# One adaLN-plus-cross-attention block: cross-attention values computed beside their own sequence, a new stage end, maxima spread by transposing a repeated column

## The chip, the cores and the metric

The kernel runs on one core of a Trainium2 chip. The metric is device time in microseconds, the median over several executions. TensorE does the matmuls and transposes, VectorE (DVE), ScalarE (ACT) and GpSimd (POOL) the elementwise work, SyncE (SP) issues most of the DMAs.

## The reference, cut to what matters

All arithmetic is float32. x has 16 sequences of 224 tokens, width 512; the context has 750 rows for each sequence; there are 16 heads of 32.

```
c_proj = silu(c) @ W_mod + b_mod                     # six rows of 512 for each sequence
shift_a, scale_a, gate_a, shift_m, scale_m, gate_m = split(c_proj, 6)
x_norm = _ln(x) * (1 + scale_a) + shift_a
q, k, v = split(x_norm @ W_qkv + b_qkv, 3)
x = x + gate_a * (softmax(q k^T * scale) v @ W_proj + b_proj)        # self-attention
q_c = _ln(x) @ W_qc + b_qc
k_c, v_c = split(_ln(context) @ W_kvc + b_kvc, 2)
x = x + (softmax(q_c k_c^T * scale) v_c @ W_cproj + b_cproj)         # cross-attention
h = gelu((_ln(x) * (1 + scale_m) + shift_m) @ W_mlp1 + b_mlp1)
x = x + gate_m * (h @ W_mlp2 + b_mlp2)
```

## The kernel before

Every engine executes its instructions in the order in which the program writes them (class Ordered), so the order of the source is the order of each queue. Tile waits for what an instruction reads or overwrites.

The program has three stages one after the other.

1. **Self-attention**, by pairs of sequences. Before it, the six conditioning parts are made from W_mod by `make_part` (line 279). Parts 0 and 1 are made before the first pair; parts 2 to 5 from slots of the plan of the first pair. For the shifts and scales it computes columns directly: for each of four output chunks and four input chunks a matmul with 128 weight columns and 16 moving columns (the profile shows two instructions for each f32 matmul). For the gates it uses c_t as weights, 16 columns, and moves 512 columns of W_mod. Parts 0 and 1 lie between c_act (the Silu of the conditioning) and the first transposes of x.

2. **Cross-attention**, by units (b, g): sequence b, group g of four heads. A unit computes scores of its six context chunks (125 rows each) in three steps; a step fills the four PSUM banks of `ps_s`, DVE keeps a running maximum in `top` and ACT copies the scores to `pt` (`keep`, line 991), which frees the banks. At the end of the unit `maxima` (line 1004) transposes `top` and reduces it to negated maxima m. One unit later the maxima are spread over the rows and added to `pt` (`subtract`, line 1031), ACT takes the exponential and POOL adds up the sums `acc` (`weights`, line 1043). Two units later the values are multiplied (`values`, line 1058) and normalized (`finish`). The spread is done so: POOL splits m into three bf16 pieces in `nmc` (`split_max`, line 122), TensorE transposes them to rows (`max_row`, line 1022), ACT copies the rows to `mrow`, and a bf16 matmul with ones puts them on all 125 partitions.

Between these steps TensorE does the other work of the stage from a plan. `at_slot(b, g, slot, f)` (line 907) puts a piece of work into one of six slots of a unit: slots 0 and 1 follow the first scores (the spread of the first half lies between them), slots 2 and 3 the second scores (the spread of the second half lies between them), slots 4 and 5 the third scores; then come the maxima of this unit, and at the start of the next unit the values of the unit before the last. The pieces are: `project_k` for the next group (slots 0 and 1), `project_q` (slot 5, in group 1 slot 3), `project_v` (values of one context chunk; chunks 0 to 3 one sequence ahead, 4 and 5 in the sequence itself), `turn_ctx` (transposes of the next sequence's context), `turn_x`, and `project` (the output projection of the sequence before, in slot 4 of groups 1 and 3). The last sequence also loads, normalizes and transposes the first rows for the MLP (`mlp_load`, `mlp_norm`, `mlp_turn`) and loads its first weights (`mlp_begin`).

After the last unit a hand-written end (lines 1106 to 1128) runs the last values, four plain MLP products, the last spread and exponentials, and the last projection.

3. **MLP**, in blocks of 512 rows, with sums of weight quarters (`mlp_sums`, line 691, and `sums_2`, line 1144) made once, while the first block runs; `First` (line 747) and `second` do the two products.

Three PSUM banks (`ps_mm`) serve all the pieces in turn, one (`ps_o`) serves the spread and the values.

Of the kernel before, what the change touches and what calls it, by code (L numbers as in the profile page):

```python
# [37 lines left out]
def kernel(  # L38
# [73 lines left out]

# [6 lines left out]
    nmc = const.tile([TP, HG, TC, P], BF16, name="nmc")  # L119
    nc.gpsimd.memset(nmc, 0.0)  # L120

    def split_max(engine, nm, m):

        r = small.tile(list(m.shape), F32, name="rest")
        engine.tensor_copy(nm[:, :, :, 0], m)
        engine.tensor_tensor(r, m, nm[:, :, :, 0], ALU.subtract)
        engine.tensor_copy(nm[:, :, :, 1], r)
        engine.tensor_tensor(nm[:, :, :, 2], r, nm[:, :, :, 1], ALU.subtract)
# [9 lines left out]
    for off, vec in ((o_mod, b_mod), (o_qkv, b_qkv), (o_qc, b_qc), (o_kvc, b_kvc), (o_mlp, b_mlp1)):  # L138
        rows = vec.shape[0] // P
        nc.scalar.dma_start(out=brow[off : off + rows, :], in_=vec.rearrange("(r p) -> r p", p=P))  # L140
# [113 lines left out]
    wq, wk, wv = (load_w(ws, w_qkv[:, i * H : (i + 1) * H], f"wqkv{i}") for i in range(3))  # L254
    bg = mp.tile([B, 2, H], F32, name="bg", bufs=1)
# [4 lines left out]
    c_act = mp.tile([B, H], F32, name="c_act", bufs=1)  # L260
    nc.scalar.activation(c_act, c_in, AF.Silu)
# [7 lines left out]
    ps = ps_mm.tile([P, 512], F32, name="mm")  # L269
    turn(ps[:, :nbias], brow, ident[:nbias, :nbias])  # L270
    nc.vector.tensor_copy(bcol, ps[:, :nbias])
    for i in (1, 4):
        sl = bcol[:, o_mod + i * KC : o_mod + (i + 1) * KC]
        nc.vector.tensor_scalar(sl, sl, 1.0, None, ALU.add)

    bqc = const.tile([P, KC], F32, name="bqc")
    nc.vector.tensor_scalar(bqc, bcol[:, o_qc : o_qc + KC], SCALE, None, ALU.mult)

    def make_part(i):
        w = w_part[i]  # L280
        ps = ps_mm.tile([P, 512], F32, name="mm")
        if i % 3 == 2:
            for k in range(KC):
                mm(ps[:B, :H], c_t[:, k, :], w[:, k, :], start=(k == 0), stop=(k == KC - 1))
            g = mp.tile([B, H], F32, name="gates", bufs=1)
            nc.vector.tensor_tensor(g, ps[:B, :H], bg[:, i // 3, :], ALU.add)
            nc.sync.dma_start(out=gate_d[i // 3], in_=g)
        else:
            slot = (i // 3) * 2 + i % 3
            for m in range(KC):  # L290
                for k in range(KC):
                    mm(
                        ps[:, m * B : (m + 1) * B], w[:, k, m * P : (m + 1) * P], c_t[:, k, :],
                        start=(k == 0), stop=(k == KC - 1),
                    )
            for m in range(KC):
                nc.vector.tensor_scalar(
                    mod_t[:, slot * KC + m, :], ps[:, m * B : (m + 1) * B],
                    bcol[:, o_mod + i * KC + m : o_mod + i * KC + m + 1], None, ALU.add,
                )  # L300
# [133 lines left out]
    if True:  # L434
# [70 lines left out]
        for p in range(NP):  # L505
            if p < NP - 1:
                for g in range(1, KC):
                    at_slot(p, 2 * g - 2, 0, lambda p=p, g=g: whole(project_qk(p, g)))
                    at_slot(p, 2 * g - 2, 1, lambda p=p, g=g: whole(project_qk(p, KC + g)))
                for t in range(PT if p else 0):  # L510
                    at_slot(p, 1 + t // 2 * 2, t % 2, lambda p=p, t=t: whole(project(p - 1, t)))
            else:

                left = [(project_qk, p, m) for m in (1, KC + 1, 2, KC + 2)]
                left += [(project, p - 1, t) for t in range(2)]
                left += [(project_qk, p, m) for m in (3, KC + 3)]
                left += [(project, p - 1, t) for t in range(2, PT)]
                parts = [h for f, *args in left for h in halves(lambda f=f, args=args: f(*args))]
                for i, h in enumerate(parts):
                    at_slot(p, i // 3, i % 3 // 2, h)  # L520
            if p == 0:
                at_slot(p, 1, 0, lambda: make_part(2))
                at_slot(p, 1, 1, lambda: make_part(3))
                at_slot(p, 1, 1, lambda: load_part(4))
                at_slot(p, 1, 1, lambda: load_part(5))
                at_slot(p, 3, 0, lambda: make_part(4))
                at_slot(p, 3, 1, lambda: make_part(5))
                at_slot(p, 3, 1, load_cross)
            n = p + 1
            if n < NP:  # L530
                if n > 1:
                    at_slot(p, 0, 0, lambda n=n: fetch(n))
                at_slot(p, 1, 0, lambda n=n: norm_begin(n))
                for t in range(PT):
                    at_slot(
                        p, 1 + t // 2, t % 2, lambda n=n, t=t: norms[PB * n + t // TC].stats(t % TC)
                    )
                for j in range(PB):
                    at_slot(p, 1 + j, 1, lambda n=n, j=j: norms[PB * n + j].apply())
                for k in range(KC):  # L540
                    at_slot(p, 4, k // 2, lambda n=n, k=k: turn_x(n, k))
                for t in range(PT):
                    at_slot(p, 5 + t // 2, t % 2, lambda n=n, t=t: project_v(n, t))
                at_slot(p, 7, 0, lambda n=n: whole(project_qk(n, 0)))
                at_slot(p, 7, 1, lambda n=n: whole(project_qk(n, KC)))

        def self_scores(p, g, j, nm):
# [15 lines left out]
            split_max(nc.vector, nm, m)  # L563
# [33 lines left out]
        make_part(0)  # L597
        make_part(1)
# [212 lines left out]
    with tc.tile_pool(name="ca", bufs=2, reuse_waits="tile") as ca:  # L811
# [98 lines left out]
        for b in range(B):  # L910
            n = b + 1
            for g in range(KC):
                f, m = (b, g + 1) if g < KC - 1 else (n, 0)
                if f < B:
                    for hf in range(2):
                        at_slot(b, g, hf, lambda f=f, m=m, hf=hf: project_k(f, m, hf))
                    at_slot(b, g, (5, 3, 5, 5)[g], lambda f=f, m=m: project_q(f, m))
            if b:
                at_slot(b, 1, 4, lambda b=b: project(b - 1, 0))
                at_slot(b, 3, 4, lambda b=b: project(b - 1, 1))  # L920
            else:
                for c in range(4):
                    at_slot(0, c // 2, 3 + c % 2, lambda c=c: project_v(0, c))
                at_slot(0, 2, 0, make_bcproj)
            at_slot(b, 0, 2, lambda b=b: project_v(b, 4))
            at_slot(b, 0, 4, lambda b=b: project_v(b, 5))
            if n < B:

                for c in range(CH):
                    at_slot(b, 0, 3 if b else 5, lambda n=n, c=c: turn_ctx(n, c))  # L930
                    at_slot(b, 2, 3, lambda n=n, c=c: turn_ctx(n, CH + c))
                for c, (u, slot) in enumerate(((1, 2), (2, 2), (2, 4), (3, 3))):
                    at_slot(b, u, slot, lambda n=n, c=c: project_v(n, c))
                for k in range(0, KC, 2):
                    at_slot(b, 3, 2, lambda n=n, k=k: turn_x(n, k))
# [5 lines left out]
            if n == B:  # L941
# [7 lines left out]
                for c, (u, slot) in enumerate(((2, 4), (2, 5), (3, 1), (3, 2))):  # L949
                    at_slot(b, u, slot, lambda c=c: mlp_turn(ps_mm, c))  # L950
            if b + 2 < B:
                for hf in range(2):
                    at_slot(b, 2 * hf, 3 if b or hf else 5, lambda b=b, hf=hf: load_ctx(b + 2, hf))
                    for c in range(CH):
                        at_slot(
                            b, 1 + 2 * hf, (4, 5, 5)[c] - hf, lambda b=b, hf=hf, c=c: cnorms[b + 2, hf].stats(c)
# [7 lines left out]
        class Unit:  # L964
# [39 lines left out]
            def maxima(self):  # L1004
                m = small.tile([TP, HG, TC], F32, name="mc")
# [14 lines left out]
                split_max(nc.gpsimd, nmc, m)  # L1020

            def max_row(self):
                ps = ps_mm.tile([P, 1024], BF16, name="mm")
                for s in range(HG):
                    for c in range(TC):
                        lo = s * N + c * TP
                        turn(ps[:, lo : lo + TP], nmc[:, s, c, :], ident16[:TP, :TP])
                self.row = ca.tile([P, HG * N], BF16, name="mrow", bufs=1)
                nc.scalar.copy(self.row, ps[:, : HG * N])

            def subtract(self, h):

                bc = ps_o.tile([P, 512], F32, name="o")
                mm(
                    bc[:CP, : 2 * N], ones16[:, :CP], self.row[:, 2 * h * N : 2 * (h + 1) * N],
                    start=True, stop=True,
                )
# [5 lines left out]
            def weights(self, h):  # L1043

                if h == 0:
# [12 lines left out]
            def values(self):  # L1058
# [7 lines left out]
                sums(self.o, [self.acc], CP)  # L1066
# [18 lines left out]
        for b, g in units:  # L1085
# [3 lines left out]
            for n in range(CH):  # L1089
                st = cur.scores(n)  # L1090
                if n == 0 and prev:
                    prev.max_row()
# [16 lines left out]
        cur.max_row()  # L1109
# [3 lines left out]
        cur.weights(0)  # L1113
        mlp_plain(sc[:, 2], 2)
        cur.subtract(1)
        cur.weights(1)
        mlp_plain(sc[:, 3], 3)
        mlp_turned(nc.vector)
        mlp_sums(nc.vector, mlp["in"], 1)
# [3 lines left out]
        cur.finish()  # L1123
        ahead = First(1)
# [7 lines left out]
    with tc.tile_pool(name="ml", bufs=3, reuse_waits="tile") as ml:  # L1132
# [32 lines left out]
        with (  # L1165
# [82 lines left out]
            for q in range(NG):  # L1248
# [64 lines left out]
```

## Time and profile before

| | |
|---|---|
| Runs before | 2943.93, 2943.95, 2952.13 us; median 2943.95 us |
| Profiled execution | 2940.97 us; span 2939.2 us; mean granted TensorE clock 0.991 |
| PE busy | 2850.1 us, 97% of the span |
| DVE, ACT, POOL busy | 65%, 40%, 44% |
| Cross-attention of sequences 1 to 14 | 854 to 2122 us of the span |
| Last sequence, stage end, first MLP block | 2122 to 2294 us |

Nearly every instruction is recorded under line 28, that of a helper, so groups are told apart by the names of their tiles: `mm<-ident,nmc` is a transpose of nmc into an mm bank. TensorE rows show the weights' partitions and columns (128*125), then the moving operand. In a timeline the columns are start, length from the first start to the last end, engine, operation, tiles, shapes, count, and in brackets the idle time before it and who ended it. Matmuls overlap, so the price of a group is the distance to the start of the next one, not its length.

### The profile page before, as it was taken

To read this page: it belongs to the slowest core of one execution; us is meant where nothing else is said; L and a number is where in the kernel's file an instruction comes from. 1 tells how busy PE (TensorE), PEld (TensorE's weight loads), DVE (VectorE), ACT (ScalarE), POOL (GpSimd) and SP (SyncE) were. 2 spreads that over 40 slices of the span, in tenths; PEclk is the share of its full clock that TensorE was granted. 3 is DMA by queue.
4 is the path that set the end of the run, shared out by engine and by line. 5 is a ranking of instruction groups with operands and counts; after the bars stand their busy time and mean duration, and the time that the engine had idled before them with its cause. 6 is when DMAs were issued, how large, how long until landed. Compare 5 with 4: busy or idle time off the path is not lost.

```text
span 2939.2 us, 46558 instructions
## 1 busy us (share of the span) xinstructions
PE 2850.1 (97%) x19389; PEld 1829.9 (62%) x19389; DVE 1913.6 (65%) x2688; ACT 1175.4 (40%) x1462; POOL 1296.2 (44%) x1636
## 2 busy tenths in 40 slices
PE   8999999998999999999999999999978999999999
PEld 5544444444555565555656555555545888888888
DVE  3677766676478778777787777777775643443343
ACT  1222222221466665666566656665653022112211
POOL 1022222122367666676666766666564510221021
PEclk9999999999999999999999999999989999999999
DMA  5111110100100010100101100000012101111110
GB/s 189 59 32 32 32 32 11 59 11 26 54 32 24 22 35 24 34 28 19 34 24 34 35 18 28 26 33 24 22 44 99 55 30 49 43 47 30 54 44 29
DMA packets 55383, 114.40 MB, mean 39 GB/s; under 512 B 4308, under 2 KB 4372, under 8 KB 55172
## 3 DMA queue, kind: packets, MB, share of 16 engines
q1 hardware_dynamic: 54560, 110.58, 11.7%
q8 instruction: 152, 2.49, 0.4%
q10 hardware_dynamic: 612, 0.85, 0.1%
q14 instruction: 59, 0.48, 0.1%
HBM read 89.33 MB, written 22.09 MB: 38 GB/s over the span
## 4 chain that ended last, share of the span: by engine, by line
PE 80%; DVE 8%; issue 4%; ACT 4%; POOL 3%; DMA 1%; SPq 0%; ACTq 0%; POOLq 0%; DVEq 0%
PE mm L28 46%; PE a L28 10%; PE sc L28 9%; PE o L28 8%; PE b L28 5%; ACT pt L28 3%; PE c L28 3%; DVE at L28 2%; DVE top L28 2%; POOL acc L28 1%; DVE stats L28 1%; DVE m L28 1%; DVE mc L28 1%; ACT kt L28 1%; DMA gate<-gate_d 1%
## 5 line engine op out<-in xcount | busy, mean ns | idle before, releaser
L28 POOL TENSOR_TENSOR acc<-acc,pt 125x448 f32<-125x448 f32 x512 | 584.3, 1141 | 40.2
L28 DVE TENSOR_TENSOR pt<-pt,o 125x896 f32<-125x896 f32 x384 | 394.4, 1082 | 92.0 <-PE o L28 87.0
L28 ACT COPY pt<-sc 125x1792 f32<-125x1792 f32 x192 | 317.4, 1653 | 223.3 <-DVE top L28 199.0
L28 DVE TENSOR_TENSOR top<-top,sc 125x896 f32<-125x896 f32 x320 | 346.7, 1084 | 40.6 <-PE sc L28 34.0
L28 PE MATMUL mm<-wkvc,cxt 128*125 128x512 f32 x768 | 354.4, 604 | 8.6 <-ACT kt L28 8.6
L28 POOL TENSOR_TENSOR upd<-upd,gate 112x512 f32<-112x512 f32 (+1 forms) x60 | 78.9, 1315 | 632.5 <-DVE upd L28 627.8
L28 PE MATMUL mm<-cxt,wkvc 128*128 128x375 f32 x1024 | 350.5, 484 | 2.4 <-ACT cxt L28 2.4
L28 ACT ACTIVATE pt<-pt 125x896 f32<-125x896 f32 x384 | 339.1, 955 | 12.9 <-DVE pt L28 12.2
L28 POOL TENSOR_TENSOR acc<-pt 125x448 f32<-125x448 f32 x128 | 146.5, 1144 | 382.6 <-ACT pt L28 382.6
L28 DVE RECIPROCAL at<-o 128x224 f32<-128x224 f32 x128 | 198.8, 1553 | 102.1 <-PE o L28 102.1
L28 PEld LDWEIGHTS mm<-cxt,wkvc 128*128 128x128 f32 x1024 | 190.4, 191 | 112.7 <-issue 13.3
L28 PEld LDWEIGHTS mm<-wkvc,cxt 128*125 128x125 f32 x768 | 136.5, 187 | 175.2 <-issue 153.5
L28 ACT ACTIVATE pt<-sc 112x1792 f32<-112x1792 f32 x64 | 106.6, 1665 | 343.4 <-PE sc L28 338.8
L28 POOL TENSOR_TENSOR rstd<-mv,eps 112x2 f32<-112x2 f32 (+3 forms) x93 | 17.8, 192 | 475.5 <-DVE mv L28 475.5
L28 PE MATMUL sc<-qt,kt 32*125 32x224 f32 x3072 | 201.6, 377 | 12.9 <-ACT pt L28 12.3
L28 PE MATMUL mm<-xt,wqkv 128*128 128x448 f32 x512 | 209.0, 551 | 4.7 <-DVE xt L28 4.7
L28 DVE TENSOR_REDUCE m<-sc 112x8 f32<-112x1792 f32 x64 | 129.6, 2026 | 120.3 <-PE sc L28 120.3
L28 PEld LDWEIGHTS sc<-qt,kt 32*125 32x125 f32 x3072 | 132.9, 183 | 92.6 <-issue 41.0
L28 ACT COPY mrow<-mm 128x896 bf16<-128x896 bf16 x64 | 58.0, 906 | 309.2 <-PE mm L28 309.2
L28 PE MATMUL o<-pt,vt 125*32 125x224 f32 x3072 | 158.6, 355 | 0.0
L28 PEld LDWEIGHTS mm<-xt,wqkv 128*128 128x128 f32 x512 | 92.3, 190 | 86.7 <-issue 80.9
L28 ACT COPY mx<-a 128x512 f32<-128x512 f32 x26 | 15.3, 587 | 325.0 <-POOL upd L28 306.3
(192 smaller groups left out, 4846.7 us busy)
## 6 DMA issues: line engine op xcount, KB each, us to landing
cx<-in_ctx_dram SPq DMA_DIRECT2D x96, 250.0 KB
x<-in_x_dram SPq DMA_DIRECT2D x16, 448.0 KB
x_self<-x SPq DMA_DIRECT2D x16, 448.0 KB
x<-x_self SPq DMA_DIRECT2D x16, 448.0 KB
x_cross<-x SPq DMA_DIRECT2D x16, 448.0 KB
mx<-x_cross SPq DMA_DIRECT2D x28, 256.0 KB
w<-in_L_xcond_W_mlp_dram SPq DMA_DIRECT2D x7, 1024.0 KB
xr<-x_cross SPq DMA_DIRECT2D x28, 256.0 KB
```

What stands on the lines that cost most here:

```text
L28: return lambda *args, **kw: self.tc.keep_in_program_order(f(*args, **kw))
```

## The change

- **Spread of the maxima.** `nmc`, the split on POOL and `max_row` go. `subtract` transposes, for each head and token chunk, the f32 column of m repeated 125 times straight into the `ps_o` bank: four transposes for each half.
- **Plan of cross-attention.** project_v of chunks 1 to 5 is done in its own sequence: group 0 slots 2, 3, 4 and group 1 slots 2, 4; only chunk 0 stays one sequence ahead (group 3 slot 4). The context is turned in group 1 slot 3 and group 2 slot 3 (before: group 0 slot 3 and group 2 slot 3), and its loads and statistics move with it. The output projection of the sequence before is in slot 2 of groups 2 and 3. project_q is in slot 5 of every group. turn_x goes to slot 3. The last sequence has its own places for the projection (group 3 slots 0 and 2) and for the MLP's transposes.
- **Stage end.** The last unit doesn't sum on POOL: TensorE sums all six pieces of pt with ones. The MLP's `mlp_turned` and `mlp_sums` on DVE come after the last unit's values and normalization, and no longer before.
- **MLP start.** `mlp_sums` of quarter 3 goes to POOL; that of quarter 0 goes from POOL to DVE, into the second product of the first block.
- **Conditioning.** The shifts and scales are computed as rows (c_t as weights, 512 columns of W_mod moved), copied by ACT and transposed in four small transposes. c_in is the first DMA on ACT's queue; the bias rows are loaded after the Silu.

The diff, cut to its core:

```diff
-    def make_part(i):
-        w = w_part[i]
+    def part_rows(i):
+
         ps = ps_mm.tile([P, 512], F32, name="mm")
+        for k in range(KC):
+            mm(ps[:B, :H], c_t[:, k, :], w_part[i][:, k, :], start=(k == 0), stop=(k == KC - 1))
+        if i % 3 < 2:
+            r = mp.tile([B, H], F32, name="part", bufs=2)
+            nc.scalar.copy(r, ps[:B, :H])
+            return r
+        return ps
+
+    def finish_part(i, ps):
...
             slot = (i // 3) * 2 + i % 3
+            rows, ps = ps, ps_mm.tile([P, 512], F32, name="mm")
             for m in range(KC):
-                for k in range(KC):
-                    mm(
-                        ps[:, m * B : (m + 1) * B], w[:, k, m * P : (m + 1) * P], c_t[:, k, :],
-                        start=(k == 0), stop=(k == KC - 1),
-                    )
+                turn(ps[:, m * B : (m + 1) * B], rows[:, m * P : (m + 1) * P], ident[:B, :B])
...
-        make_part(0)
-        make_part(1)
+        rows = [part_rows(i) for i in range(2)]
+        make_columns()
+        for i in range(2):
+            finish_part(i, rows[i])
...
-                    at_slot(b, g, (5, 3, 5, 5)[g], lambda f=f, m=m: project_q(f, m))
+                    at_slot(b, g, 5, lambda f=f, m=m: project_q(f, m))
             if b:
-                at_slot(b, 1, 4, lambda b=b: project(b - 1, 0))
-                at_slot(b, 3, 4, lambda b=b: project(b - 1, 1))
+                for c, (u, slot) in enumerate(((2, 2), (3, 2)) if n < B else ((3, 0), (3, 2))):
+                    at_slot(b, u, slot, lambda b=b, c=c: project(b - 1, c))
             else:
-                for c in range(4):
-                    at_slot(0, c // 2, 3 + c % 2, lambda c=c: project_v(0, c))
-                at_slot(0, 2, 0, make_bcproj)
-            at_slot(b, 0, 2, lambda b=b: project_v(b, 4))
-            at_slot(b, 0, 4, lambda b=b: project_v(b, 5))
+                at_slot(0, 0, 2, lambda: project_v(0, 0))
+                at_slot(0, 2, 2, make_bcproj)
+            for c, (u, slot) in enumerate(((0, 2), (0, 3), (0, 4), (1, 2), (1, 4))):
+                at_slot(b, u, slot, lambda b=b, c=c + 1: project_v(b, c))
             if n < B:
                 for c in range(CH):
-                    at_slot(b, 0, 3 if b else 5, lambda n=n, c=c: turn_ctx(n, c))
+                    at_slot(b, 1, 3, lambda n=n, c=c: turn_ctx(n, c))
                     at_slot(b, 2, 3, lambda n=n, c=c: turn_ctx(n, CH + c))
-                for c, (u, slot) in enumerate(((1, 2), (2, 2), (2, 4), (3, 3))):
-                    at_slot(b, u, slot, lambda n=n, c=c: project_v(n, c))
+                at_slot(b, 3, 4, lambda n=n: project_v(n, 0))
                 for k in range(0, KC, 2):
-                    at_slot(b, 3, 2, lambda n=n, k=k: turn_x(n, k))
+                    at_slot(b, 3, 3, lambda n=n, k=k: turn_x(n, k))
...
-                for c, (u, slot) in enumerate(((2, 4), (2, 5), (3, 1), (3, 2))):
+                for c, (u, slot) in enumerate(((2, 2), (2, 3), (2, 4), (3, 4))):
                     at_slot(b, u, slot, lambda c=c: mlp_turn(ps_mm, c))
             if b + 2 < B:
                 for hf in range(2):
-                    at_slot(b, 2 * hf, 3 if b or hf else 5, lambda b=b, hf=hf: load_ctx(b + 2, hf))
+                    at_slot(b, 1 + hf, 3, lambda b=b, hf=hf: load_ctx(b + 2, hf))
                     for c in range(CH):
                         at_slot(
-                            b, 1 + 2 * hf, (4, 5, 5)[c] - hf, lambda b=b, hf=hf, c=c: cnorms[b + 2, hf].stats(c)
+                            b, 2 + hf, (4, 5, 5)[c] - hf, lambda b=b, hf=hf, c=c: cnorms[b + 2, hf].stats(c)
                         )
...
             def subtract(self, h):
                 bc = ps_o.tile([P, 512], F32, name="o")
-                mm(
-                    bc[:CP, : 2 * N], ones16[:, :CP], self.row[:, 2 * h * N : 2 * (h + 1) * N],
-                    start=True, stop=True,
-                )
+                for s in range(2):
+                    for c in range(TC):
+                        lo = s * N + c * TP
+                        col = self.m[:, 2 * h + s, c : c + 1].to_broadcast([TP, CP])
+                        turn(bc[:CP, lo : lo + TP], col, ident[:TP, :TP])
...
-                sums(self.o, [self.acc], CP)
+                if self.acc is None:
+                    sums(self.o, [pt[:, :, j * N : (j + 1) * N] for pt in self.pts for j in range(2)], CP)
+                else:
+                    sums(self.o, [self.acc], CP)
...
         mlp_plain(sc[:, 0], 0)
-        cur.max_row()
         prev.finish()
         mlp_plain(sc[:, 1], 1)
         cur.subtract(0)
-        cur.weights(0)
+        cur.weights(0, False)
         mlp_plain(sc[:, 2], 2)
         cur.subtract(1)
-        cur.weights(1)
+        cur.weights(1, False)
         mlp_plain(sc[:, 3], 3)
-        mlp_turned(nc.vector)
-        mlp_sums(nc.vector, mlp["in"], 1)
         for m in range(KC):
             gelu(sc[:, m], mlp["h"][0][:, m], m)
         cur.values()
         cur.finish()
+        mlp_turned(nc.vector)
+        mlp_sums(nc.vector, mlp["in"], 1)
...
-                    mlp_sums(nc.vector, ml, 3)
+                    mlp_sums(nc.gpsimd, ml, 3)
                     sums_2()
                     first(3)
-                    mlp_sums(nc.gpsimd, ml, 0)
...
+                    if (i, half, p) == (GC, 0, 3):
+                        mlp_sums(nc.vector, ml, 0)
```

More of the change, by code (lines that the diff above doesn't have):

```diff
@@ L117, with split_max @@
         nms.append(t)
-    nmc = const.tile([TP, HG, TC, P], BF16, name="nmc")
-    nc.gpsimd.memset(nmc, 0.0)
-    def split_max(engine, nm, m):
+    def split_max(nm, m):
         r = small.tile(list(m.shape), F32, name="rest")
[L125 to L128, printed above, removed]
+        nc.vector.tensor_copy(nm[:, :, :, 0], m)
+        nc.vector.tensor_tensor(r, m, nm[:, :, :, 0], ALU.subtract)
+        nc.vector.tensor_copy(nm[:, :, :, 1], r)
+        nc.vector.tensor_tensor(nm[:, :, :, 2], r, nm[:, :, :, 1], ALU.subtract)
     o_mod, o_qkv = 0, 6 * KC
@@ L137 @@
     brow = const.tile([nbias, P], F32, name="brow")
-    for off, vec in ((o_mod, b_mod), (o_qkv, b_qkv), (o_qc, b_qc), (o_kvc, b_kvc), (o_mlp, b_mlp1)):
-        rows = vec.shape[0] // P
-        nc.scalar.dma_start(out=brow[off : off + rows, :], in_=vec.rearrange("(r p) -> r p", p=P))
     bcol = const.tile([P, nbias], F32, name="bcol")
@@ L254 @@
     wq, wk, wv = (load_w(ws, w_qkv[:, i * H : (i + 1) * H], f"wqkv{i}") for i in range(3))
+    c_act = mp.tile([B, H], F32, name="c_act", bufs=1)
+    nc.scalar.activation(c_act, c_in, AF.Silu)
+    for off, vec in ((o_mod, b_mod), (o_qkv, b_qkv), (o_qc, b_qc), (o_kvc, b_kvc), (o_mlp, b_mlp1)):
+        rows = vec.shape[0] // P
+        nc.scalar.dma_start(out=brow[off : off + rows, :], in_=vec.rearrange("(r p) -> r p", p=P))
     bg = mp.tile([B, 2, H], F32, name="bg", bufs=1)
@@ L258 @@
         nc.scalar.dma_start(out=bg[:, i, :], in_=b_mod[lo : lo + H].partition_broadcast(B))
-    c_act = mp.tile([B, H], F32, name="c_act", bufs=1)
-    nc.scalar.activation(c_act, c_in, AF.Silu)
     c_t = mp.tile([P, KC, B], F32, name="c_t", bufs=1)
@@ L267, with make_columns @@
     nc.vector.tensor_copy(c_t.rearrange("p k b -> p (k b)"), ps[:, : KC * B])
[L269 to L274, printed above, removed]
     bqc = const.tile([P, KC], F32, name="bqc")
-    nc.vector.tensor_scalar(bqc, bcol[:, o_qc : o_qc + KC], SCALE, None, ALU.mult)
-    def make_part(i):
-        w = w_part[i]
+    def make_columns():
         ps = ps_mm.tile([P, 512], F32, name="mm")
+        turn(ps[:, :nbias], brow, ident[:nbias, :nbias])
+        nc.vector.tensor_copy(bcol, ps[:, :nbias])
+        for i in (1, 4):
+            sl = bcol[:, o_mod + i * KC : o_mod + (i + 1) * KC]
+            nc.vector.tensor_scalar(sl, sl, 1.0, None, ALU.add)
+        nc.vector.tensor_scalar(bqc, bcol[:, o_qc : o_qc + KC], SCALE, None, ALU.mult)
+    def part_rows(i):
+        ps = ps_mm.tile([P, 512], F32, name="mm")
+        for k in range(KC):
[6 more added lines that the diff above has]
+    def finish_part(i, ps):
         if i % 3 == 2:
-            for k in range(KC):
-                mm(ps[:B, :H], c_t[:, k, :], w[:, k, :], start=(k == 0), stop=(k == KC - 1))
             g = mp.tile([B, H], F32, name="gates", bufs=1)
@@ L289, in make_part @@
             slot = (i // 3) * 2 + i % 3
+            rows, ps = ps, ps_mm.tile([P, 512], F32, name="mm")
             for m in range(KC):
-                for k in range(KC):
-                    mm(
-                        ps[:, m * B : (m + 1) * B], w[:, k, m * P : (m + 1) * P], c_t[:, k, :],
-                        start=(k == 0), stop=(k == KC - 1),
-                    )
+                turn(ps[:, m * B : (m + 1) * B], rows[:, m * P : (m + 1) * P], ident[:B, :B])
             for m in range(KC):
@@ L521, with part @@
             if p == 0:
-                at_slot(p, 1, 0, lambda: make_part(2))
-                at_slot(p, 1, 1, lambda: make_part(3))
+                made = {}
+                def part(i):
+                    made[i] = part_rows(i)
+                    if i % 3 == 2:
+                        finish_part(i, made[i])
+                at_slot(p, 1, 0, lambda: part(2))
+                at_slot(p, 1, 1, lambda: part(3))
                 at_slot(p, 1, 1, lambda: load_part(4))
                 at_slot(p, 1, 1, lambda: load_part(5))
-                at_slot(p, 3, 0, lambda: make_part(4))
-                at_slot(p, 3, 1, lambda: make_part(5))
+                at_slot(p, 2, 0, lambda: finish_part(3, made[3]))
+                at_slot(p, 3, 0, lambda: part(4))
+                at_slot(p, 3, 1, lambda: part(5))
+                at_slot(p, 3, 1, lambda: finish_part(4, made[4]))
                 at_slot(p, 3, 1, load_cross)
@@ L562, in self_scores @@
             )
-            split_max(nc.vector, nm, m)
+            split_max(nm, m)
         def self_weights(p, g, j, row):
@@ L1004, in maxima @@
             def maxima(self):
-                m = small.tile([TP, HG, TC], F32, name="mc")
+                self.m = m = small.tile([TP, HG, TC], F32, name="mc")
                 for h in range(2):
@@ L1019, in maxima, with subtract @@
                     )
[L1020 to L1024, printed above, removed]
+            def subtract(self, h):
+                bc = ps_o.tile([P, 512], F32, name="o")
+                for s in range(2):
                     for c in range(TC):
                         lo = s * N + c * TP
[L1027 to L1033, printed above, removed]
-                mm(
-                    bc[:CP, : 2 * N], ones16[:, :CP], self.row[:, 2 * h * N : 2 * (h + 1) * N],
-                    start=True, stop=True,
-                )
+                        col = self.m[:, 2 * h + s, c : c + 1].to_broadcast([TP, CP])
+                        turn(bc[:CP, lo : lo + TP], col, ident[:TP, :TP])
                 less = bc[:CP, : 2 * N].rearrange("p (s t) -> p s t", s=2).unsqueeze(2)
@@ L1041, in subtract, with weights @@
                     nc.vector.tensor_tensor(w4, w4, less.to_broadcast([CP, 2, 2, N]), ALU.add)
-            def weights(self, h):
+            def weights(self, h, add=True):
+                if not add:
+                    for pt in self.pts:
+                        w = pt[:, 2 * h : 2 * h + 2, :]
+                        nc.scalar.activation(w, w, AF.Exp)
+                    self.acc = None
+                    return
                 if h == 0:
@@ L1090 @@
                 st = cur.scores(n)
-                if n == 0 and prev:
-                    prev.max_row()
                 if n == 0 and last:
```

## The prediction

> **What bounds the kernel now.** The page first: is one engine the bound over the whole span?
>
> ```profile
> PE 2850.1 (97%) x19389; PEld 1829.9 (62%) x19389; DVE 1913.6 (65%) x2688; ACT 1175.4 (40%) x1462; POOL 1296.2 (44%) x1636
> ```
>
> TensorE is. So a change pays only where it takes work from TensorE, ends one of its waits, or keeps its clock up. Where its idle time lies is in the table by stretches (columns: stretch, its length, busy us of PE, PEld, DVE, ACT, POOL, granted clock, DMA share, GB/s):
>
> ```profile
> 750.00:854.00 104.00, 98.76 (x642) 57.04 (x642) 64.88 (x87) 53.00 (x63) 52.21 (x75) 0.98 0.12 38
> 854.00:2122.00 1268.00, 1250.10 (x9530) 751.55 (x9532) 976.27 (x1137) 783.09 (x924) 869.71 (x1114) 1.00 0.08 26
> 2122.00:2217.60 95.60, 75.85 (x608) 46.12 (x600) 72.99 (x98) 49.57 (x51) 57.66 (x72) 0.89 0.15 49
> 2217.60:2255.50 37.90, 30.65 (x134) 15.46 (x131) 21.92 (x20) 10.90 (x13) 15.24 (x14) 0.91 0.04 13
> 2255.50:2294.00 38.50, 34.66 (x154) 29.99 (x153) 22.57 (x22) 12.46 (x27) 22.34 (x10) 0.96 0.60 200
> ```
>
> These are cross-attention of sequence 0, of 1 to 14, of 15, the stage's end, and the first MLP block. The middle sequences (90.54 us each) leave TensorE 18 us idle in all; sequence 15 and what follows leave 31 us in 172, at a lowered clock. The waits of TensorE between 800 and 2100 us name what small stalls there are:
>
> ```profile
> PE mm L28 <- POOL nmc L28: 8.5, 14, 0.6
> PE mm L28 <- ACT kt L28: 8.1, 14, 0.6
> ```
>
> Last, the timeline of TensorE and VectorE through one unit (sequence 4, group 2; start, length, what):
>
> ```profile
> 1091.32 0.35 PE L28 MATMUL o<-mrow,ones 128*125 128x448 bf16 x1
> 1091.51 1.57 PE L28 MATMUL mm<-ident,cx 125*128 125x125 f32 x12
> 1093.01 1.04 PE L28 MATMUL sc<-qt,kt 32*125 32x224 f32 x16
> 1093.97 3.70 PE L28 MATMUL mm<-wkvc,cxt 128*125 128x512 f32 x8
> 1097.51 1.68 PE L28 MATMUL mm<-xt,wqc 128*128 128x224 f32 x8
> 1099.02 1.02 PE L28 MATMUL mm<-ident,top 125*112 125x125 f32 x8
> ```
>
> ```profile
> 1091.71 3.08 DVE L28 TENSOR_TENSOR pt<-pt,o 125x896 f32<-125x896 f32 x3 [1.58 <-PE o L28]
> 1094.71 2.21 DVE L28 TENSOR_TENSOR top<-top,sc 125x896 f32<-125x896 f32 x2
> ```
>
> TensorE has no gap, and the next start is the true price of a group: 3.54 us for project_v, 1.50 for turn_ctx, 0.97 for scores, 1.51 for project_q, 0.95 for the maxima's turns, then 2.79 for values and sums. The top maximum, which the turns need, was done at 1096.92, 2.1 us ahead of need. That spare time matters below.
>
> **The change part by part** (us; minus is saved).
>
> **1. Spread of the maxima.** Per unit it removes eight bf16 turns (0.40), two bf16 matmuls with ones (0.19 each), an ACT copy (0.91) and four POOL operations (about 1.2 with gaps). ACT and POOL are not the bound there. It adds eight f32 turns of a repeated column, 112 columns moved. Nearest row, starts 0.82 us apart with one bank change inside:
>
> ```profile
> 1110.49 0.98 PE L28 MATMUL mm<-ident,xn 112*128 112x112 f32 x8
> 1111.32 0.35 PE L28 MATMUL o<-mrow,ones 128*125 128x448 bf16 x1
> ```
>
> So 0.77 to 0.82 comes for 0.78: between 0 and +0.04 per unit, +2 over 64 units. No row shows a weight load from one repeated element; if it costs what the other f32 turns pay it hides behind the 96 ns step. The Trainium skill, TensorE: Matmul & The Clock Gate, section LDWEIGHTS, prices a load by its columns alone, at columns/1.2 ns, which is 104 ns for 125: an estimate of +4 more. I take the trace's 96 ns; the upper end is in the first rival. Turns now wait for DVE's m alone; m is there a whole slot earlier.
>
> **2. Middle sequences, 1 to 14.** Today each loses 1.88 us of TensorE: after group 1's first scores 0.70 (nmc), 0.35 at that group's top and query, in group 3 0.83 (kt evicted late). The change ends these: no nmc; group 1 gets values (a 3.5 us cover) before the turns; group 3's projection covers kt. Against that, group 2 becomes bare: slot 2 project (3.5), slot 3 turn_ctx, slot 4 no TensorE work, slot 5 project_q. From the spread (t=0) DVE adds the projection's bias first (until 0.8), subtracts three times (until 3.8), takes two maxima (until 6.0). TensorE needs 0.4 + 1.5 + 0.97 + 1.51 = 4.4 and waits 1.7 us. POOL's sums, 5.95 us from the first exponential, then hold the last matmuls another 0.2. So +1.9 against -1.88: +1 over 14 sequences. Moving values out and project in is otherwise even, 3.5 against 3.5.
>
> Would the clock fall in this wait? The same page, section PE-mode transpose, says that transposes don't count as busy for the gate. By it the 1.9 us and 0.95 us of turns leave a 3.4 us window nearly empty, the clock halves for one window, and each sequence pays 1.7: +24. But here the turns from 23.98 to 27.00 ran 0.19 us apart and the matmuls behind them at full speed, 0.375 apart: turns alone raised the clock. I take 0 and keep +24 as a rival.
>
> **3. Sequences 0 and 15.** Three project_v (10.6 us) move from 0 to 15. Sequence 0 is 103.96 now. By the same queues its groups become 24.7, 27.4 (POOL's acc behind cx applies stays the end), 23.7 (bcproj waits for DVE's rep, then the bare slot), 21.5: -6.5. Sequence 15 is 96.06. It takes the 10.6 us in its idle time: 24.8, 25.9 (POOL: norms ahead of acc, as now), 23.6 (three mlp_turns on DVE, but spread 4 us earlier), 21.0: -0.7.
>
> **4. Stage end.** Now sums waits for POOL's acc, and the clock drops:
>
> ```profile
> 2241.69 0.96 PE L28 MATMUL o<-acc,ones 125*32 125x224 f32 x4 [6.46 <-POOL acc L28]
> 2242.58 5.22 PE L28 MATMUL mm<-mxt,w 128*128 128x256 f32 x16
> ```
>
> 37.9 us from 2217.6. New: four mlp_plain and two spreads 14.9; values 2.3; sums over six pieces 2.3 in place of 0.5; First.begin 3.5 (it reads no region that mlp_turned writes); project 3.5; then DVE, which has done normalize, turned and sums (eight operations of 0.7 to 0.9), evicts at 29.1; project 3.5: 32.6. That is -5.3; the 2.6 us wait may halve the clock once, so -4.7.
>
> **5. MLP start.** mlp_sums(3) leaves DVE for POOL, which sits idle till the first w2 lands at 2268.9. Four POOL operations of 1.66 end near 2272.4, ahead of need at 2279.7. Removed:
>
> ```profile
> 2283.71 3.39 PE L28 MATMUL a<-tt,ws 128*128 128x256 f32 x8 [3.84 <-DVE ws L28]
> ```
>
> With the half-speed window behind it: 5.73 + 3.23 - 2x1.73 = -5.5. sums_2 starts 3.5 later but ends at the same w2 landings, about 2292, before 2295. mlp_sums(0) on DVE (four of 0.7) is covered by a stage where DVE is 42% busy; uncovered it costs 2.8.
>
> **6. Conditioning rows.** At the start:
>
> ```profile
> 10.30 13.84 PE L28 MATMUL mm<-c_t,w_mod 128*128 128x16 f32 x64
> 23.98 3.18 PE L28 MATMUL mm<-ident,xn 112*128 112x112 f32 x16
> ```
>
> c_in is now sixth on ACT's DMA queue and TensorE starts at 9.4. The first DMA on that queue, issued at 0.72, landed by 2.1, and the first w_mod by 5.7 (the trace's landing marks), so matmuls can start at 5.9. The seven bias DMAs (about 0.4 each, bg 3) are issued behind Silu from 3 us, and are needed at 16. Sixteen dense matmul passes replace 64 small ones that kept the clock half: about 4 us at 0.85, the rest at 0.43, with a wait for the second w_mod (near 12.7, an estimate from the GB/s of the first 13 us), end 16.2; ACT copy, turns, mod_t, eight modulates of 0.43 as now: the first qk ends at 22.7, not 30.0. I take -7.0 (-4 if c_in lands as late as now). Later, parts 3 and 4 (3.70 each, even in work) each pull the clock down:
>
> ```profile
> 64.53:67.94 3.41, 3.41 (x43) 3.12 (x46) 1.92 (x6) 0.54 (x1) 0.00 (x0) 1.00 0.86 286
> 67.94:71.36 3.42, 3.42 (x30) 1.74 (x19) 1.51 (x3) 0.00 (x0) 2.31 (x6) 0.50 0.90 284
> ```
>
> Part 2, already dense, does not (57.7 to 64.5 at 1.00). Two half-speed windows less: -3.2. The new copies on ACT (0.6) and turns are small beside an idle ACT.
>
> **Sum:** +2 +1 -6.5 -0.7 -4.7 -5.5 -7.0 -3.2 = -24.6. The profiled execution took 2940.97 (span 2939.2 and 1.8 around): 2916.4. The median shown is 2943.95, 3.0 above it; on it the forecast is 2919.4, say 2919.
>
> **The rivals.**
> - **Repeated column loads slowly (slower).** One mechanism: 512 weight loads from a single element. A plain f32 load of 128 columns records 190 ns (the page's PEld rows); not hidden, each turn takes 0.19 instead of 0.096: +48 us, 2967. The gain is gone at 0.144 a turn, slower past the bound at 0.161. Against: all f32 turns load at the step of their 112 or 125 columns. Chance 0.10.
> - **The clock falls in group 2.** +24: 2943, no change. For: 1.9 us idle in 3.4; windows with about a third busy fell. Against: this one is 44% busy. Chance 0.12.
> - **Ends gain half.** The start is bound by landings, sequence 15 by POOL: -12, 2932. Chance 0.18.
> - **Group 2 doesn't wait** because DVE runs ahead: -14 more, 2905. Chance 0.10.
> - **Reordering brings a wait I don't see,** past the gain: 0.03.
>
> **How the numbers follow.** The main case has 0.47, at 2919 (2908 to 2930). About 0.3% (9 us) is what a measurement of this kernel can tell from no change. Faster: 0.47 + 0.18 + 0.10 and 0.02 of the clock case at its better edge, 0.77. Same: the other 0.10 of the clock case and 0.01 of the first rival, 0.11. Slower: 0.09 of the first and 0.03 of the last, 0.12. The range takes the fourth case, the ends and the clock case: 2902 to 2945.
>
> **What would show it.** Right: first qk ends near 23; no half clock at 68 and 85; no POOL nmc or acc wait above 1 us at the stage end; a wait of 1.7 for top in every group 2, at clock 1.00; turns 96 ns apart. Wrong: turns at 0.15 or more; clock 0.5 windows in the middle sequences; sequence 15 above 100 us.

## The result, and the profile after

The changed kernel takes 2964.82 us (median, 2960.27 to 2965.02) where the kernel before takes 2943.95: the ratio is 1.0059, 95% interval 1.0043 to 1.0075, slower by about 21 us. The prediction said 2919, with a range of 2902 to 2945. The profiled execution has a span of 2963.2 us, 24.0 above that of before. The engine line, and the same stretches as before (sequence 0, sequences 1 to 14, sequence 15, the stage's end, the first MLP block; columns as in the first table of that kind):

```profile
PE 2856.9 (96%) x19221; PEld 1831.3 (62%) x19221; DVE 1903.5 (64%) x2688; ACT 1121.6 (38%) x1402; POOL 1224.6 (41%) x1369
```

```profile
744.91:846.76 101.85, 90.21 (x608) 53.65 (x608) 66.38 (x87) 48.17 (x57) 52.48 (x67) 0.97 0.12 36
846.76:2150.26 1303.50, 1260.74 (x9412) 768.74 (x9409) 977.89 (x1136) 734.47 (x868) 818.07 (x881) 1.00 0.08 27
2150.26:2250.21 99.95, 86.25 (x629) 51.32 (x625) 73.59 (x98) 48.14 (x50) 54.81 (x58) 0.91 0.11 37
2250.21:2282.03 31.82, 30.29 (x173) 15.70 (x170) 16.43 (x20) 9.99 (x12) 1.27 (x1) 1.00 0.00 1
2282.03:2314.84 32.81, 32.81 (x154) 28.88 (x153) 11.72 (x17) 12.35 (x27) 22.12 (x12) 1.00 0.68 232
```

The last two lines are the gains that were forecast: 37.9 became 31.8, and 38.3 (from the first tt product; the line of before began at another boundary) became 32.8. The second line is the loss. The 14 middle sequences took 1267.6 us, counted from first scores to first scores, and take 1303.5; TensorE, which lacked 18 us there, now lacks 43. The median one costs 93.16 instead of 90.54. The two longest waits of TensorE between 800 and 2140 us (us in total, times, longest), where before had nmc and kt:

```profile
PE mm L28 <- DVE top L28: 24.0, 15, 1.6
PE mm L28 <- ACT vt L28: 20.0, 27, 1.2
```

The first is the wait that the prediction expected in group 2; the second it did not have at all. Two timelines show them. First group 2 of sequence 4, the group that the prediction read in the kernel before (its lines lie in sequence 3, by the count that starts at 0; the middle sequences are alike):

```profile
1185.72 0.59 PE L28 MATMUL o<-ident,mc 112*125 112x112 f32 x4
1185.92 0.69 DVE L28 TENSOR_TENSOR upd<-mm,bcproj 112x512 f32<-112x512 f32 x1 [1.38 <-PE mm L28]
1186.15 1.45 PE L28 MATMUL mm<-ident,cx 125*128 125x125 f32 x12
1186.53 3.07 DVE L28 TENSOR_TENSOR pt<-pt,o 125x896 f32<-125x896 f32 x3
1188.49 1.78 PE L28 MATMUL mm<-xt,wqc 128*128 128x224 f32 x8
1189.52 2.20 DVE L28 TENSOR_TENSOR top<-top,sc 125x896 f32<-125x896 f32 x2
1191.87 1.04 PE L28 MATMUL mm<-ident,top 125*112 125x125 f32 x8 [1.60 <-DVE top L28]
```

DVE works without a gap from the projection's bias to the top maximum, 6.0 us after the spread; TensorE has 4.4 us of work and then stands still for 1.6. The forecast wait was 1.7. Then group 3 of the same sequence:

```profile
1207.39 0.93 PE L28 MATMUL mm<-ident,xn 112*128 112x112 f32 x8
1209.21 3.70 PE L28 MATMUL mm<-wkvc,cxt 128*125 128x512 f32 x8
1211.58 2.17 DVE L28 TENSOR_TENSOR top<-top,sc 125x896 f32<-125x896 f32 x2
1213.87 1.65 ACT L28 COPY pt<-sc 125x1792 f32<-125x1792 f32 x1 [2.04 <-DVE top L28]
1214.26 0.59 PE L28 MATMUL mm<-ident,top 125*112 125x125 f32 x4
1215.41 0.59 ACT L28 COPY vt<-mm 125x512 f32<-125x512 f32 x1
1216.06 0.64 PE L28 MATMUL mm<-ident,top 125*112 125x125 f32 x4 [1.21 <-ACT vt L28]
```

TensorE's first four turns of top start at 1214.26 without a wait for top, which was done at 1213.75. The second four need another PSUM bank. The three mm banks are used in turn: project_v took one, project_q the next, the first four turns the third, so the second four need project_v's again. Its values were complete by 1212.9, but ACT copies them out only at 1215.41: ahead of that copy in ACT's order is the copy of the third scores to pt, and that one started when DVE's top was done. Both only read the scores, and no run shows why the copy waits for the maximum; the profile of before names the same pair:

```profile
ACT pt L28 <- DVE top L28: 199.0, 175, 3.4
```

### The profile page after: what moved, and what is told of

Its sections match the earlier page's. It is cut to its first block, busy times and chain, and to the rows that moved or that the text cites. A ratio compares the mean times of both kernels' runs of the same rounds, so it can differ in the third digit from the quotient of the medians.

```text
span 2963.2 us, 45946 instructions
## 1 busy us (share of the span) xinstructions
PE 2856.9 (96%) x19221; PEld 1831.3 (62%) x19221; DVE 1903.5 (64%) x2688; ACT 1121.6 (38%) x1402; POOL 1224.6 (41%) x1369
## 4 chain that ended last, share of the span: by engine, by line
PE 80%; DVE 11%; issue 4%; ACT 3%; POOL 2%; DMA 1%; SPq 0%; POOLq 0%; ACTq 0%; DVEq 0%
PE mm L28 42%; PE o L28 10%; PE sc L28 10%; PE a L28 10%; PE b L28 5%; DVE pt L28 3%; DVE top L28 3%; PE c L28 2%; ACT pt L28 2%; DVE at L28 1%; DVE m L28 1%; DVE upd L28 1%; POOL acc L28 1%; POOL upd L28 1%; DMA gate<-gate_d 0%
## 5 line engine op out<-in xcount | busy, mean ns | idle before, releaser
L28 POOL TENSOR_TENSOR acc<-acc,pt 125x448 f32<-125x448 f32 x504 | 573.2, 1137 | 39.5
L28 DVE TENSOR_REDUCE mc<-mm 112x4 f32<-112x500 f32 x128 | 82.9, 669 | 106.0 <-PE mm L28 105.9
```

Source lines behind the costliest of these rows:

```text
L28: return lambda *args, **kw: self.tc.keep_in_program_order(f(*args, **kw))
```

## The experiments

The theory: the plan costs the time, in two ways (a bare slot 4 in group 2, and the vt copy behind the pt copy on ACT in groups 1 and 3); the ends gain as forecast. The rivals: the new spread costs it, or the turns wait for top itself, or the ends' gain is taken back anyway.

**Plan, spread and ends taken apart.** Four kernels: after with the old plan (the core of its edit is below); and before with one part of the change each: the new spread, the new plan, or the new ends (conditioning rows, stage end, quarter 3's sums on POOL).

```diff
-                at_slot(b, 1, 3, lambda n=n, c=c: turn_ctx(n, c))
+                at_slot(b, 0, 3 if b else 5, lambda n=n, c=c: turn_ctx(n, c))
...
-                at_slot(b, 3, 4, lambda n=n: project_v(n, 0))
+                for c, (u, slot) in enumerate(((1, 2), (2, 2), (2, 4), (3, 3))):
+                    at_slot(b, u, slot, lambda n=n, c=c: project_v(n, c))
```

> The changed kernel with the plan of cross-attention of before put back (project_v, turn_ctx, project, project_q, turn_x, the MLP's turns and the context's loads in their old slots); the new spread, the stage end, the MLP start and the conditioning rows stay. Theory (the plan costs the time): a middle sequence falls from 93.17 to about 90 us (88.7 of TensorE's work, 0.5 for the longer spread, 0.8 for the late kt of group 3), 14 of them 42 to 46 us, sequence 15 from 100 to 96: 2915 to 2925 us. Rival (the spread's turns, or DVE's maxima feeding them, cost the time): the middle sequences stay above 92.5, 2950 or more.

> The kernel before with the new spread of the maxima alone. Theory (the plan costs the time): a spread group of four turns costs 0.42 us where the old one cost 0.19 and a share of 0.20, +0.5 a sequence in all, and the 0.70 us wait for nmc in group 1 goes: 2935 to 2945 us. Rival (the spread costs): +2.6 a sequence here too, about 2980 us.

> The kernel before with the new plan of cross-attention alone: spread, stage end, MLP start and conditioning of before. Theory (the plan's loss stands by itself): the 47 us between the changed kernel and the one with the plan put back, on top of 2943: 2985 to 2995 us. Rival (the loss needs the new spread too, whose turns wait for DVE's m instead of POOL's nmc): under 2970 us.

> The kernel before with the conditioning rows, the new stage end and mlp_sums of quarter 3 on POOL; plan and spread of before, and mlp_sums of quarter 0 on POOL as before. Theory (the ends gain, the cross-attention loses): 5 to 8.5 us at the start, 6.1 at the stage end, 5.5 at the MLP's start: 2924 to 2928 us. Rival (what the ends gain is taken back by a later wait whatever the middle does, as the self-attention's gain shrank from 8.5 to 5.1 us): 2934 or more.

Measured, against before in the same sessions (2942.7 to 2942.9):

| kernel | us | ratio, 95% interval | a middle sequence (median) |
|---|---|---|---|
| after, old plan | 2917.53 | 0.9909 (0.9896 to 0.9923) | 89.98 |
| before, new spread | 2931.54 | 0.9961 (0.9948 to 0.9975) | 89.98 |
| before, new plan | 2990.49 | 1.0154 (1.0136 to 1.0171) | 92.94 |
| before, new ends | 2925.78 | 0.9937 (0.9925 to 0.9950) | 90.55 |

The plan alone costs 47.6 us, the spread gains 11.1, the ends gain 16.9: together +19.6. The whole change measured +20.9; it also moves quarter 0's sums to DVE, which is in none of the three parts and is priced below. The sum is near and not exact: in the profile of the plan alone 6.8 us of the loss lie ahead of the first cross scores (756.8 instead of 750.0), where its code is that of before. The first row prices the plan without that: 47.3 between the changed kernel and the one with the old plan, whose profiles start the stage at 744.9 and 745.7. By either the plan costs more than the whole change lost. The spread did better than its expectation of 2935 to 2945: not only does the nmc wait go, the kt wait in group 3 shrinks a little too. In the kernel with the old plan this is the only wait left in the middle sequences:

```profile
PE mm L28 <- ACT kt L28: 6.4, 14, 0.5
```

**The copy of vt.** The changed kernel; only the ACT copy of the third scores is issued behind slot 4.

```diff
...
                 cur.keep(n, st)
                 run(plan, (b, g, 2 * n))
+                if n == CH - 1:
+                    cur.copy(st)
```

> The changed kernel, and only the ACT copy of the third scores to pt is issued after slot 4 and no longer before it, so that the copy of vt made in slot 4 doesn't stand behind it on ACT. Theory (DVE's top is late, ACT's pt copy waits for it, the vt copy stands behind that and holds the bank that the second half of the maxima's turns needs): the waits of 0.5 in group 1 and 1.4 in group 3 go, 1.9 x 14 = 27 us: 2935 to 2942 us; the 1.9 of group 2 stays. Rival (the turns wait for top itself): nothing goes, 2960 to 2968 us.

Measured: 2938.44 us, ratio to before 0.9983 (0.9976 to 0.9989), 26 us below the changed kernel. Of the two lines of waits in the middle sequences one is left, and group 3 of sequence 4 shows the two copies exchanged and eight turns in one piece:

```profile
PE mm L28 <- DVE top L28: 22.4, 14, 1.6
```

```profile
1203.16 2.17 DVE L28 TENSOR_TENSOR top<-top,sc 125x896 f32<-125x896 f32 x2
1204.54 0.58 ACT L28 COPY vt<-mm 125x512 f32<-125x512 f32 x1 [1.12 <-PE mm L28]
1205.43 1.65 ACT L28 COPY pt<-sc 125x1792 f32<-125x1792 f32 x1 [0.31 <-DVE top L28]
1205.85 1.02 PE L28 MATMUL mm<-ident,top 125*112 125x125 f32 x8
```

DVE's work and TensorE's work are the same as before the exchange; only ACT's order differs. Group 1 falls from 23.44 to 22.92 and group 3 from 23.60 to 22.19: 1.93 a sequence. The rival, that the turns wait for top itself, is out for these two groups.

**The bare slot.** project_v spread evenly, so that every slot 4 holds one; first alone, then with the late copy (and with mlp_sums of quarter 0 back on POOL).

```diff
...
-            for c, (u, slot) in enumerate(((0, 2), (0, 3), (0, 4), (1, 2), (1, 4))):
-                at_slot(b, u, slot, lambda b=b, c=c + 1: project_v(b, c))
+            for c, (u, slot) in enumerate(((0, 2), (0, 4), (1, 2), (1, 4))):
+                at_slot(b, u, slot, lambda b=b, c=c + 2: project_v(b, c))
...
-                at_slot(b, 3, 4, lambda n=n: project_v(n, 0))
+                at_slot(b, 2, 4, lambda n=n: project_v(n, 0))
+                at_slot(b, 3, 4, lambda n=n: project_v(n, 1))
```

> The changed kernel with project_v spread evenly: chunks 0 and 1 one sequence ahead in slot 4 of groups 2 and 3, chunks 2 and 3 in group 0 slots 2 and 4, chunks 4 and 5 in group 1 slots 2 and 4, so that no slot 4 is bare. Theory (two losses: the bare slot 4, and the vt copy behind the pt copy on ACT): the 1.9 us wait of group 2 goes, but group 0 has now an empty slot 3 and about 0.8 us of the vt wait comes there, while those of groups 1 and 3 stay: about 1.2 a sequence, 17 us, 2944 to 2952 us. Rival (the bare slot is all of it, so all 2.6 us a sequence go): 2925 to 2932.

> The changed kernel with all three losses taken away: the even places of project_v, the ACT copy of the third scores behind slot 4, and mlp_sums of quarter 0 on POOL. Theory: a middle sequence is TensorE's own work, 88.7 + 0.5 = 89.2 to 89.5 us; 14 of them 52 to 55 us less than the changed kernel, 2.7 at the MLP: 2903 to 2912 us, below every other kernel. Rival (a bare slot or a late copy reappears elsewhere, or the values' own place costs something that is not seen as a wait): 90 us or more, 2915 to 2925.

Alone: 2953.32 us, a little above the expected 2944 to 2952. The wait for top is gone, and this has grown in its place:

```profile
PE mm L28 <- ACT vt L28: 32.8, 41, 1.5
```

Group 0, whose slot 3 is now empty, has joined groups 1 and 3. With the late copy: 2911.28 us, and a middle sequence takes 89.34; the list of waits for the middle sequences is empty. So the two losses are separate. Of the 3.82 us by which the changed kernel's sequence is longer, groups 0 and 2 together account for 1.89, group 1 for 0.52, group 3 for 1.41.

**The sums of quarter 0.** Behind the first MLP block the changed kernel lost 2.9 us at one place, a product that waits for DVE's sums of h:

```profile
2336.53 0.68 DVE L28 TENSOR_TENSOR ws<-w 128x512 f32<-128x512 f32 x1
2336.70 1.64 POOL L28 TENSOR_TENSOR upd<-upd,gate 128x512 f32<-128x512 f32 x1 [1.03 <-DVE upd L28]
2337.25 1.64 DVE L28 TENSOR_TENSOR w<-w 128x512 f32<-128x512 f32 x1
2338.42 1.60 POOL L28 TENSOR_TENSOR xr<-xr,upd 128x512 f32<-128x512 f32 x1
2338.82 1.75 DVE L28 TENSOR_TENSOR ws<-ws,w 128x512 f32<-128x512 f32 x1
2350.10 1.99 PE L28 MATMUL a<-wcproj,h 128*128 128x256 f32 x8 [2.71 <-DVE h L28]
```

Two of the four sums took 1.64 and 1.75 instead of 0.68, beside POOL's additions. Two kernels try other places: POOL behind the first block (with the old plan), and DVE in part 6 of the second half (with the even plan and the late copy).

```diff
                     first(3)
+                    mlp_sums(nc.gpsimd, ml, 0)
...
-                    if (i, half, p) == (GC, 0, 3):
-                        mlp_sums(nc.vector, ml, 0)
```

```diff
-                    if (i, half, p) == (GC, 0, 3):
+                    if (i, half, p) == (GC, 1, 6):
                         mlp_sums(nc.vector, ml, 0)
```

> The kernel with the plan put back (the first experiment), and mlp_sums of quarter 0 on POOL behind the first MLP block as before, no longer on DVE in the second product. Theory (DVE's sums delay the operands of the next block's product, 2.7 us of TensorE): 2.7 us less than with the plan put back, 2914 to 2916 us. Rival (POOL is then late for something in the first block instead): no gain, 2917 to 2920.

> The kernel with even places and the late copy, but mlp_sums of quarter 0 neither on POOL behind the first block nor on DVE in its third product: on DVE in the sixth part of the second half, where POOL has little to do and no product waits for DVE's sums of h. Theory (DVE and POOL slow each other when both add f32 in SBUF, 0.69 us against 1.6 to 2.7 us in the traces, and TensorE then waits for h): the 4.0 us of waits at t2's products go, 2907 to 2909 us. Rival (the wait is for POOL's sums of w2, moved back by the sums of quarter 3): stays at 2911.

On POOL: 2914.29 us, 3.2 below the kernel with the old plan, as expected, but in part by luck: in the two profiles 2.8 us of the difference lie ahead of sequence 15, where both run the same code, and the wait only moved. POOL's sums of w2 and of quarter 0 now lie beside DVE's sums of h for the first half, which take up to 2.7 us each, and the first product with t2 waits 2.2. In part 6 of the second half, where POOL is idle, the four sums take 0.68 to 0.69 each, nothing waits for them, and what follows the first block (from the first product with h) takes 645.4 us, as before (645.4; changed kernel 648.4). The place changed together with what runs beside it, so this doesn't set the slowing apart from the four additions themselves. By estimate the slowing of two of the four (1.64 and 1.75 where 0.68 is enough) makes 2.0 of the 2.9. This kernel measured 2908.52 us, ratio to before 0.9878 (0.9864 to 0.9893): the fastest here. Its middle sequences (TensorE 1250.3 of 1250.8 us):

```profile
846.90:2097.70 1250.80, 1250.26 (x9412) 771.21 (x9408) 975.24 (x1136) 739.33 (x868) 822.06 (x885) 1.00 0.09 28
```

**Is it the repetition that makes a turn longer?** The trace has 0.106 us for a turn of the spread where the prediction took 0.096.

```diff
-                        col = self.m[:, 2 * h + s, c : c + 1].to_broadcast([TP, CP])
+                        col = self.m[:, :CP]
```

> The kernel before with the new spread, but each turn loads 125 real columns of a wider tile (the maxima in the first eight, zeros behind) and no longer one column repeated 125 times; it adds numbers that aren't the maxima. Theory (a repeated column loads like any other, and the step of 0.106 us is that of 125 columns): turns stay at 0.105 to 0.107 us and the time within 2 us of 2931.5. Rival (the repeated element makes the step longer than the 0.096 us of the other 112-row turns): 0.096 us a turn, 512 x 0.010 = 5 us less.

Measured: the turns stay at 0.106 us, four in 0.42, and a middle sequence at 89.99, so the repetition costs nothing. The median was 2935.59, 4 us above the kernel with the repeated column and outside the 2 us expected. The profile has it outside cross-attention: the first cross scores start at 756.8 instead of 750.9, behind half-speed windows at the end of self-attention, which differ between profiles of the same start.

**A mixed plan.** Sequences 0 and 15 in their old slots, the rest even.

```diff
+            edge = b in (0, B - 1)
...
+                beside = ((1, 2), (2, 2), (2, 4), (3, 3)) if b == 0 else ((2, 2), (2, 4), (3, 2), (3, 4)) if n == B - 1 else ((2, 4), (3, 4))
```

> The same, with the old plan in sequences 0 and 15: four chunks of values ahead in sequence 0 (sequence 1 computes two itself), four in sequence 14 for 15 (beside the projections and in slot 4 of groups 2 and 3), context, x, projection and MLP turns of those two in their old slots. Theory (the old sequence 15 was bound by POOL and DVE, not by TensorE's work, and sequence 0 had idle time for the values of the next): sequence 0 falls from 104.0 to 102, sequence 15 from 97.2 to 94, 2902 to 2905 us. Rival (sequence 1 with two values fewer has too little work to cover DVE, and sequence 14 pays in full): equal to the even plan or above, 2907 to 2912.

Measured: 2911.76 us. The rival was right: sequence 15 falls to 92.2, but sequence 14 takes 96.2 (two values more) and sequence 1 takes 92.4 with two fewer, at a clock that fell twice. Sequence 0 takes 103.3 and not the 102 hoped for. The values ahead of the last sequence aren't free.

## Why the prediction was wrong, step by step

| stretch, us | predicted change | after less before |
|---|---|---|
| up to the first cross scores | -10.2 | -5.1 |
| sequence 0 | -6.5 | -2.1 |
| sequences 1 to 14 | +3 (with the spread) | +35.9 |
| sequence 15 | -0.7 | +3.9 |
| stage end | -4.7 | -6.1 |
| first MLP block | -5.5 | -5.5 |
| behind it | 0 | +3.0 |

**Step 2 failed, and with it the forecast.** Its wait in group 2 came as computed (1.9 a sequence, clock 1.00 over the stretch). But for group 1 it said only that the values give "a 3.5 us cover", and for group 3 that "projection covers kt": TensorE's work was counted and DVE's queue was followed in one group of four. In the kernel before, group 3 had this between the spread of the second half and the third scores:

```profile
1112.25 3.70 PE L28 MATMUL mm<-wkvc,cxt 128*125 128x512 f32 x8 [0.58 <-ACT kt L28]
1115.88 1.04 PE L28 MATMUL sc<-qt,kt 32*125 32x224 f32 x16
```

In the changed kernel turn_x (0.86) took the place of this project_v (3.54), while DVE got the projection's bias in front of its subtractions. So top came later relative to TensorE, and the pt copy, the vt copy and the bank with it. In group 1 turn_ctx brought no less work to slot 3, but project_v came into slot 4, where before the projection was, whose result DVE takes and not ACT; the x statistics stand ahead of top there, as they did before. This is the rival "reordering brings a wait I don't see", which had 0.03 and no price. Its price was 1.9 a sequence, 27 us of the 33 by which the middle sequences missed. Without it the changed kernel measures 2938: a little faster than before, and 19 above the forecast.

**Step 3** failed too, mostly by other waits. Groups 0 and 1 came as forecast (24.65 and 27.65 in sequence 0, 24.87 and 25.95 in sequence 15); group 2 took 26.4 and 26.1 instead of 23.7 and 23.6, group 3 23.2 and 23.0 instead of 21.5 and 21.0. In sequence 0 the product for bcproj waits for DVE's rep, a wait that the step named, and behind turn_x in group 3 the third scores wait for the ACT copy of the second scores, which it didn't; the clock falls behind each.

```profile
PE mm L28 <- DVE rep L28: 3.4, 1, 3.4
PE sc L28 <- ACT pt L28: 2.7, 1, 2.7
```

The late copy doesn't mend these two sequences: with it they take 101.0 and 101.5 us, where the changed kernel took 101.9 and 100.0. What holds group 2 of sequence 15 stays open.

**Step 1** had the right mechanism and a size that was too small. Alone, the new spread shortens a middle sequence by 0.56 us. By the starts of the groups the waits fall by 0.80 (0.70 at nmc, 0.10 at kt), so its own work costs 0.24, or 0.06 a unit where 0 to 0.04 was said. Four turns take 0.42, the two groups of project_k beside them grow (2.63 and 2.64, from 2.59 and 2.62), and two groups of turn_ctx shrink (1.38, from 1.50). The rule that was set aside, LDWEIGHTS of the Trainium skill (TensorE: Matmul & The Clock Gate), gives 104 ns for 125 columns and was nearer to the 106 here; it doesn't explain the 96 ns of xn's turns with 128 columns, so why one shape steps at 96 and the other at 106 stays open.

**Steps 4 and 6 held, and step 5 but for its last term.** Stage end: sums over six pieces take 2.39 us and nothing waits for acc.

```profile
2267.43 2.45 PE L28 MATMUL o<-pt,ones 125*32 125x224 f32 x48
2269.82 3.72 PE L28 MATMUL mm<-mxt,w 128*128 128x256 f32 x16
2278.50 3.69 PE L28 MATMUL sc<-wcproj,at 128*112 128x512 f32 x8 [1.53 <-DVE upd L28]
```

The last wait was put at 2.6, and the clock, which was to halve once, did not. The MLP start gained 5.5 to a tenth. At the start the matmuls begin at 6.37 (forecast 5.9), and the first qk begins 6.8 us earlier:

```profile
6.37 5.46 PE L28 MATMUL mm<-w_mod,c_t 128*16 128x512 f32 x8 [1.06 <-DMA w_mod<-in_L_xcond_W_mod_dram]
20.20 6.25 PE L28 MATMUL mm<-xt,wqkv 128*128 128x448 f32 x16 [0.22 <-PE mm L28]
```

The half-speed windows at 68 and 85 are gone; at 692 us the lead is 8.5. By the first cross scores 5.1 is left, because the kernel before happened to lose less clock there (granted 0.90 over 700 to 750 us; 0.81 in the changed kernel over 692 to 745): with the old start the first cross scores came at 750.0, 750.9, 756.8 and 756.8 in four kernels, with the new one between 742.2 and 745.7 in nine. The means differ by 9.6, close to the 10.2 of the forecast, though each kernel gave one profile.

**Step 5's cover** for mlp_sums(0) was argued from an average ("DVE is 42% busy") and was not there. Its uncovered price of 2.8 came out (2.87), but by luck: it counted four additions of 0.7, and DVE ran beside POOL. The Trainium skill (SBUF — State Buffer, section "Who interferes with whom") says that a DVE instruction with two SBUF inputs contends with a GpSimd instruction that reads SBUF. The trace agrees: 1.64 and 1.75 us beside POOL, 0.68 when POOL is idle. Weighing this in the step might have put the sums elsewhere.

The other rivals: the repeated column loads slowly is out (0.106, under the 0.144 at which the gain ends); the clock falls in group 2 is out (granted clock 1.00 over sequences 1 to 14, and the eight turns behind the wait take 1.04 us where before they took 1.02); the stage end and the MLP start gained what they were to gain, the start only as a mean. A label in step 2 was off, without effect on its sum: the nmc wait follows the first scores of group 2, for the maxima of group 1.

## What to carry to other kernels

When work moves between slots, follow every engine's queue through every slot that changed: the copy that frees a bank waits behind whatever its engine was given earlier, and that may wait for a third engine. A slot's worth as cover is the work left between the releasing step and the next wait, so compare what stands there before and after (3.5 us became 0.9), not the total per sequence. Then a small reordering, here one ACT copy, can return what a plan lost.

## What the runs showed of the hardware

An f32 addition of 128x512 on DVE takes 0.68 us alone and 1.6 to 2.7 beside an addition on POOL, which itself goes from 1.27 to 1.6 or more. A wait of 1.6 us ahead of a group of turns did not lower the granted clock (1.00 in the middle sequences, 14 times). That column alone is not enough: at 23.57 to 26.98 us of the kernel before it reads 1.00 while turns step at 0.19 us, twice the usual, so the step is worth reading too. Half-speed windows at the end of self-attention moved the first cross scores by up to 6.8 us (750.0 to 756.8) between kernels with the same self-attention, so one pair of profiles can't price a change ahead of such a place.
